# Deriving due times of the first groups' layers and weights from their users in a four-layer graph network

## The chip, the cores and the metric

The kernel runs on one core of one Trainium2 chip. The metric is the device time of one execution in microseconds (us); lower is better. Before the change it is 1435.51 us, the median of 3 runs (1435.34 to 1436.21). A core has a matrix engine (TensorE, PE in the profile, with its weight loads shown apart as PEld), a vector engine (VectorE, DVE), an activation engine (ScalarE, ACT), GpSimd (POOL), and SyncE (SP), whose queue issues the loads and stores here.

## The reference, cut to what matters

The input is 128 graphs of 64 nodes with 256 features, each with its own 64x64 adjacency. Four layers follow each other, each in the form x = x + layer(relu(layernorm(x)), adj):

```python
# layer 0: attention with 4 heads        e = leaky_relu(e_src_i + e_dst_j); masked softmax; alpha @ (h W); elu
# layer 1: the same with one head
# layer 2: relational convolution; adj holds only 0 and 1, so one relation of 40 is left:
#          (adj^T == 1) @ ((h W^T + b) * sigmoid(h W^T Wg^T + bg)), then relu
# layer 3: three steps of a gated recurrence with shared gates
for i in range(3):
    m = einsum("bnd,de->bne", h, weight[i])
    aggr = einsum("bst,bsd->btd", A, m)
    h = gru_cell(aggr, h, w_ih, w_hh, b_ih, b_hh)
```

All arithmetic is in float32. No graph needs another one, so the order of the graphs is free.

## The kernel before

Two graphs fill the 128 partitions, and four such pairs form a group (G = 4): 16 groups of 512 rows. For each group the kernel runs `first_layer`, `second_layer` (both call `attention`, line 1097) and `third_layer` (`loop_relation`, line 1187), then `before` (layernorm and transposes for the recurrence, line 739) and `recur` (`recurrence`, line 757: three steps with two halves of the features each). Groups 0 and 1 go through the layers in two halves of two pairs. For them layernorm's transposes run on PE; later groups (`g >= AHEAD`, line 1003) transpose by DVE and DMA. The second half of group 0 uses buffers of its own, with names that end in `e`.

The weights are prepared at the start. `later_weights` (line 1161) makes `wl` for the third layer from W_loop and Wg_loop (tiles `wn`, `gn`), `whh` from `hhn`, and for each of the three steps `wc`, a product of the transposed step weight (`gT`) and the transposed input weight (`ihT`). The step weights are loaded into `wrn0` and into the single buffers `wn` and `gn`, which they share with W_loop and Wg_loop: whichever load comes second waits until the first one's readers are done. The recurrence's buffers take the memory of the preparation (`make_gru`, line 1238), so all preparation and the halves of group 0 with an `e` must be done before recurrence 0 places a tile.

The code does not issue instructions in the order in which it is written. `Plan` (line 208) records each operation with an estimated cost, and `emit` (line 267) writes them out by list scheduling. It keeps a clock for each engine and takes the operation that can start first; where several of one engine are ready, it takes the one with the earliest due time (`key = (t, op.due)`, line 333). A result that another engine needs counts as ready `LATENCY` ns after its end. Each operation belongs to a job, opened by `begin`. A job with a start and an end spreads its operations' due times over that stretch; a job without an end counts back from the users:

```python
            if op.job.end is None:
                op.due = min((t.due for t in op.then), default=1e9) - op.cost
            else:
                op.due = (op.job.end - (op.job.end - op.job.start) * op.tail / op.job.length) * 1e3
```

The stretches are written by hand from line 1253 on: the weights from 18.0 to 79.1 us, the layers of groups 0 and 1 in `units`, recurrence g from `start + g * period` with start 93.6 and period 83.8. The chip then runs each engine's list in this fixed order.

Where the planner sees PE wait before 115 us, it puts filler products of a constant tile there (`nc.spare`, line 1315, `ni<-warm` in the profile). Their bank `ni` is later one of the five PSUM banks that only the recurrence uses (`Banks`, line 953); until a recurrence places its first tile in one of those five, the flag `early` is true and other tiles may use four of them.

In the profile nearly every instruction has line 384, the helper that records operations; products issued as a bundle have line 605. So tiles tell them apart: `mm<-w0e`, `mm<-w1e` and `mm<-wl` are the layers' products, `mm<-ihT,gT` makes wc, and `ry`, `rm`, `rz`, `nh`, `ni` belong to the recurrence.

Of the kernel before, what the change touches and what calls it, by code (L numbers as in the profile page):

```python
# [20 lines left out]
G = 4  # L21
# [27 lines left out]
class View:  # L49


    def __init__(self, base, shape, steps=(), region=None, live=None):
        self.base, self.shape, self.steps, self.region, self.live = base, tuple(shape), steps, region, live
# [83 lines left out]
class Pool:  # L137
# [3 lines left out]
    psum = False  # L141
# [21 lines left out]
    def released(self, tag, base, before):  # L163
# [3 lines left out]
        if before < 0:  # L167
            return 0.0
        return sorted(b.end for b in live if not b.left)[before] + Plan.LATENCY

# [29 lines left out]
class Job:  # L200
# [2 lines left out]

    def __init__(self, start, end, after):
        self.start, self.end, self.after, self.left, self.length = start, end, after, 0, 0.0


class Plan:

    LATENCY = 164.2

    def __init__(self, nc):
        self.nc, self.on, self.ops, self.job = nc, False, [], None
# [51 lines left out]
    def emit(self):  # L267
# [19 lines left out]
            op.job.length = max(op.job.length, op.tail)  # L287
        for op in reversed(self.ops):
            if op.job.end is None:
                op.due = min((t.due for t in op.then), default=1e9) - op.cost  # L290
            else:
                op.due = (op.job.end - (op.job.end - op.job.start) * op.tail / op.job.length) * 1e3
        free = dict.fromkeys([*ENGINES.values(), "-"], 0.0)
# [5 lines left out]
        def enter(op):  # L299
            t = 0.0  # L300
            for other, data in op.after.items():
                late = other.end + self.LATENCY
                if other.engine == op.engine and not (other.dma and data):
# [9 lines left out]
        while left:  # L313
            best = None
            for e, ops in ready.items():
                found = None
                for op in ops:
                    t = max(free[e], op.ready)
# [5 lines left out]
                    for b in op.needs:  # L324
                        if b.real is None:
# [5 lines left out]
                            t = max(t, b.pool.released(tag, b, taken.count(tag)))  # L331
# [7 lines left out]
            t, _, op, places = best  # L339
# [34 lines left out]
class Engine:  # L374
# [3 lines left out]
    def __getattr__(self, method):  # L378
        plan, engine = self.plan, self.name
        do = getattr(getattr(plan.nc, engine), method)  # L380

        def call(*args, **kwargs):
            def emit():
                return do(*[real(a) for a in args], **{k: real(v) for k, v in kwargs.items()})  # L384

            if not plan.on:
                return emit()
            writes = [v for v in args[:1] if isinstance(v, View)]
            reads = [v for v in [*args[1:], *kwargs.values()] if isinstance(v, View)]
            plan.note(  # L390
                ENGINES[engine], emit, cost(engine, method, args, kwargs), writes, reads,
                port=port(engine, method, writes, reads), dma=method == "dma_start",
            )

        return call
# [45 lines left out]
def kernel(  # L441
# [28 lines left out]
    nc = Plan(tc.nc)  # L470
# [128 lines left out]
    def beside(products, cost):  # L599

        def emit():
            for product in products:
                nc.nc.tensor.matmul(*[real(x) for x in product], start=True, stop=True)  # L605

        if not nc.on:
            return emit()
        writes = list({id(x[0].base): x[0] for x in products}.values())
        nc.note("PE", emit, cost, [Plan.all_of(x) for x in writes], [x for p in products for x in p[1:]])  # L610
# [337 lines left out]
    with ExitStack() as s1:  # L948
# [34 lines left out]
        psum = Banks(s1.enter_context(tc.tile_pool(name="psum", bufs=1, space=PSUM)), 1, Banks.own)  # L983
# [29 lines left out]
        def load_group(g):  # L1013
            nc.begin(("load", g))
            xg = work.tile([P, G, D], F32, name="xg", bufs=6)
            n = 2 if g == 0 else G
            for p in range(0, G, n):
                nc.sync.dma_start(xg[:, p : p + n], xr[:, g * G + p : g * G + p + n, :])
            at = work.tile([P, G // 2, 2, N], I32, name="at", bufs=3)
            for a in range(2):  # L1020
                for u in range(G // 2):
                    edges = tr[g * G // 2 + u, a]
                    nc.sync.dma_start(at[a * N : (a + 1) * N, u], edges)
            AT.append(at)
            XG.append(xg)
# [131 lines left out]
        def first_weights():  # L1157
            attention_columns(w0e, H, (AB[:, 0, :], AB[:, 1, :]))
            attention_columns(w1e, 1, (AB[:, 2, :], AB[:, 3, :]))
# [82 lines left out]
        def before(g):  # L1242
            ABD[g] = work.tile([P, G, N], F32, name="abd")
            START[g] = before_recurrence(W[3], psum, XG[g], AG[g], ABD[g], g >= AHEAD)

        def recur(g):
            recurrence(
                W[3], psum, START.pop(g), XG[g], ABD[g],
                lambda h, part: nc.sync.dma_start(outr[:, g * G : (g + 1) * G, :][part], h[part]),
                g == NG - 1,  # L1250
            )

        nc.begin("columns")
        first_weights()
        nc.begin("weights", 18.0, 79.1)
        later_weights(early)
        layers = (first_layer, second_layer, third_layer)
        start, period = 93.6, 83.8
        users = {}
        for g in range(NG):  # L1260
            if g > 1:
                load_group(g)

            if g == 0:
                units = [(0, 2, (-2.5, 24.3, 61.4, 71.1)), (2, 2, (-2.7, 25.3, 58.8, 74.4))]
            elif g == 1:
                units = [(0, 2, (27.5, 54.4, 87.5, 95.7)), (2, 2, (45.3, 71.4, 100.6, 129.4))]
            elif g == 2:
                units = [(0, G, (72.8, 119.1, 176.7, 238.7))]
            else:  # L1270
                end = start + g * period - 26.2
                units = [(0, G, [end - 53.5 * i + x for i, x in ((3, 0.0), (2, 0.0), (1, 0.0), (0, 0.0))])]
            for p0, n, at in units:
                spare = g == 0 and p0 > 0
                for i in range(3):
                    nc.begin((g, p0, i), at[i], at[i + 1], [users[i]] if i in users and not spare else [])
                    if not spare:
                        users[i] = (g, p0, i)
                    layers[i](g, p0, n, spare)
            if g == 0:  # L1280
                nc.begin("make")
                nc.note("-", make_gru, 0.0, [], [], [op for op in nc.ops if any(b.pool is early for b in op.bases)])
            at = start + g * period
            nc.begin(("before", g), at - (13.0 if g == 0 else 22.3), at, [("recur", g - 2)] if g > 1 else [])
            before(g)
            nc.begin(("recur", g), at, at + period)
            recur(g)
# [23 lines left out]
        if 115.0:  # L1311
            warm = const.tile([P, P], F32, name="warm")
            nc.nc.vector.memset(warm, 1.0)
            pause = psum.real.tile([P, P], F32, name="ni", tag="ni", bufs=1)
            nc.spare = lambda: nc.nc.tensor.matmul(pause, warm, warm, start=True, stop=True)  # L1315
        with tc.manual_schedule(engines={getattr(mybir.EngineType, e) for e in ENGINES.values()}):
            nc.emit()

# [214 lines left out]
```

## Time and profile before

| | us |
|---|---|
| time, median of 3 | 1435.51 |
| span of the profiled execution | 1432.5 |
| PE idle in the first 100 us | 2.06 |
| first product of recurrence 0 (ry) | 112.98 |
| first product of recurrence 1, of 2 | 197.12, 280.55 |
| last recurrence's last product starts | 1421.83 |

The span is the time from the first to the last instruction of one profiled execution on this core. The page gives busy time of each engine, the granted clock of PE in 40 slices, the chain of waits that ended last, and groups of instructions by line, operation and tile. Other views of the same trace show stretches of time, the order of instructions, or who waited for whom. A float32 product is two records (passes) in the trace, while the program has one instruction; counts after "x" in the profile are records unless a line says otherwise. Ends of products are modelled, so neighbouring products overlap in the records; the distance between starts gives the time that a product takes in a row of products.

### The profile page before, as it was taken

What the parts mean: (1) busy time and instruction counts of PE and PEld (TensorE: products, weight loads), DVE (VectorE), ACT (ScalarE), POOL (GpSimd) and SP (SyncE); (2) the same over time, 40 slices, a digit from 0 to 9 for tenths busy, and PEclk for the clock granted to TensorE, in tenths of its full rate; (3) what the DMA queues carried; (4) which work ended last, traced back from release to release, by engine and by line L of the source; (5) the groups of instructions that cost most, each with busy time, mean ns of one, the idle gap of its engine ahead of it and who ended that gap; (6) DMA issues with size and microseconds to landing.
All of it is one profiled execution on the core that took longest, in us unless ns stands there. A gap on an engine that the chain in (4) does not pass through costs nothing.

```text
span 1432.5 us, 28063 instructions
## 1 busy us (share of the span) xinstructions
PE 1412.5 (99%) x9779; PEld 973.6 (68%) x9779; DVE 1041.5 (73%) x2745; ACT 778.7 (54%) x1853; POOL 597.7 (42%) x744
## 2 busy tenths in 40 slices
PE   9999999999999999999999999999999999999997
PEld 9676676666667666666766666676666667666664
DVE  5568688686867878686887868688686868774544
ACT  3654655555565565556555555655655555554543
POOL 1424624534434453443445344344534434452422
PEclk9999999999999999999999999999999999999999
DMA  7010221222223122222312222231212222110000
GB/s 214 19 27 24 38 60 30 47 53 52 60 43 75 28 51 54 52 60 44 77 25 51 54 52 60 43 76 27 46 39 48 46 42 58 25 34 15 16 16 18
DMA packets 299421, 67.91 MB, mean 47 GB/s; under 512 B 274696, under 2 KB 297480, under 8 KB 299272
## 3 DMA queue, kind: packets, MB, share of 16 engines
q1 hardware_dynamic: 298712, 65.50, 21.7%
q8 instruction: 81, 1.33, 0.4%
q10 hardware_dynamic: 560, 0.52, 0.1%
q14 instruction: 68, 0.56, 0.1%
HBM read 28.06 MB, written 8.53 MB: 26 GB/s over the span
## 4 chain that ended last, share of the span: by engine, by line
PE 88%; DVE 4%; SPq 3%; ACT 3%; DMA 1%; issue 1%; POOL 1%; DVEq 0%; POOLq 0%; ACTq 0%
PE ry L384 22%; PE mm L384 16%; PE rz L384 11%; PE ni L384 11%; PE nh L384 10%; PE rm L384 5%; PE tp L384 4%; PE mm L605 3%; SPq L384 3%; PE tp L605 2%; PE ni L1315 2%; DVE d L384 1%; POOL d L384 1%; DVE hT L384 1%; DMA t<-row 1%
## 5 line engine op out<-in xcount | busy, mean ns | idle before, releaser
L384 POOL TENSOR_TENSOR d<-hT,t 128x256 f32<-128x256 f32 x192 | 151.9, 798 | 487.7 <-ACT t L384 486.8
L384 PE MATMUL ni<-aT,wc 128*128 128x512 f32 x384 | 194.1, 592 | 0.0
L384 PE MATMUL nh<-hT,whh 128*128 128x512 f32 x384 | 193.8, 593 | 0.2 <-DVE hT L384 0.2
L384 ACT ACTIVATE z<-z,brz 128x256 f32<-128x256 f32 x192 | 97.4, 507 | 155.9 <-DVE z L384 155.3
L384 DVE SCALAR_TENSOR_TENSOR d<-z,d 128x256 f32<-128x256 f32 x192 | 127.2, 669 | 58.1 <-POOL d L384 45.2
L384 POOL TENSOR_TENSOR hS<-hT 128x256 f32<-128x256 f32 x96 | 73.9, 770 | 175.5 <-PE ry L384 136.3
L384 ACT COPY z<-ry 128x256 f32<-128x256 f32 x192 | 71.2, 371 | 126.4 <-PE ry L384 91.2
L384 DVE SCALAR_TENSOR_TENSOR t<-r,t 128x256 f32<-128x256 f32 x192 | 98.0, 511 | 50.2 <-ACT r L384 44.5
L384 DVE TENSOR_TENSOR z<-rz,z 128x256 f32<-128x256 f32 x192 | 80.2, 418 | 59.1 <-PE rz L384 46.6
L384 PE MATMUL rz<-hS,whh 128*128 128x256 f32 x384 | 119.5, 393 | 1.1 <-DVE z L384 1.0
L384 PE MATMUL mm<-wl,hT 128*128 128x512 f32 x248 | 118.1, 598 | 0.0
L384 PE MATMUL ry<-hS,wsum 128*128 128x256 f32 x384 | 115.9, 383 | 0.8 <-ACT z L384 0.8
L384 PE MATMUL rz<-aS,wc 128*128 128x256 f32 x384 | 115.6, 383 | 0.0
L384 PE MATMUL ry<-aS,wsum 128*128 128x256 f32 x384 | 114.2, 379 | 0.0
L384 ACT ACTIVATE hn<-xg,var,rstd 128x256 f32<-128x256 f32 x200 | 107.1, 592 | 9.9 <-DVE var L384 9.8
L384 ACT ACTIVATE t<-t,bi 128x256 f32<-128x256 f32 x192 | 93.8, 502 | 19.8 <-DVE t L384 19.2
L384 PEld LDWEIGHTS ry<-hS,wsum 128*128 128x128 f32 x384 | 70.0, 190 | 47.0 <-issue 32.0
L384 DVE BATCH_NORM_STATS2 st<-xg 128x6 f32<-128x256 f32 x256 | 98.5, 413 | 3.2 <-DMA xg<-in_x_dram 2.5
L384 DVE SCALAR_TENSOR_TENSOR hT<-d,t 128x256 f32<-128x256 f32 x192 | 91.9, 485 | 6.1
L384 POOL TENSOR_TENSOR rstd<-var,mhalf 128x4 f32<-128x4 f32 (+1 forms) x70 | 68.7, 984 | 56.4 <-DVE var L384 47.4
L384 PEld LDWEIGHTS nh<-hT,whh 128*128 128x128 f32 x384 | 70.1, 190 | 27.3 <-issue 17.4
L384 PEld LDWEIGHTS ry<-aS,wsum 128*128 128x128 f32 x384 | 73.0, 190 | 22.7 <-issue 10.3
(203 smaller groups left out, 3227.6 us busy)
## 6 DMA issues: line engine op xcount, KB each, us to landing
hT<-hn SPq DMA_DIRECT2D x896, 32.0 KB
xg<-in_x_dram SPq DMA_DIRECT2D x15, 512.0 KB
out_dram<-hnat SPq DMA_DIRECT2D x15, 512.0 KB
t<-row SPq DMA_DIRECT2D x28, 256.0 KB
at<-in_adj_dram SPq DMA_DIRECT2D x64, 32.0 KB
eg<-in_adj_dram SPq DMA_DIRECT2D x64, 32.0 KB
ag<-in_adj_dram SPq DMA_DIRECT2D x16, 128.0 KB
t<-row SPq DMA_DIRECT2D x28, 64.0 KB
```

The source lines that it names most:

```text
L384: return do(*[real(a) for a in args], **{k: real(v) for k, v in kwargs.items()})
L605: nc.nc.tensor.matmul(*[real(x) for x in product], start=True, stop=True)
L1315: nc.spare = lambda: nc.nc.tensor.matmul(pause, warm, warm, start=True, stop=True)
```

## The change

Due times of the weights and of the layers of groups 0 and 1 are no longer spread over hand-written stretches. Their jobs have no end now, so each operation is due as late as its users allow, counted back through the operations to the recurrences, whose stretches keep fixed times. In the count, the cost of each operation, and LATENCY where the user sits on another engine, are multiplied by 1.76 (`spread`). The start is now 86.2 and the period 83.85, LATENCY 170.8, and the dates of the later groups are set anew. Filler products are emitted only while `early` is true, so that none is written into a bank of a recurrence.

```diff
         self.start, self.end, self.after, self.left, self.length = start, end, after, 0, 0.0
+        self.spread = 1.76
...
-    LATENCY = 164.2
+    LATENCY = 170.8
...
             if op.job.end is None:
-                op.due = min((t.due for t in op.then), default=1e9) - op.cost
+                op.due = 1e9
+                for t in op.then:
+                    late = 0.0 if t.engine == op.engine else self.LATENCY
+                    op.due = min(op.due, t.due - op.job.spread * (op.cost + late))
...
-        nc.begin("weights", 18.0, 79.1)
+        nc.begin("weights", 18.0, 0 or None)
...
-        start, period = 93.6, 83.8
+        start, period = 86.2, 83.85
...
             elif g == 1:
-                units = [(0, 2, (27.5, 54.4, 87.5, 95.7)), (2, 2, (45.3, 71.4, 100.6, 129.4))]
+                units = [(0, 2, (24.1, 54.4, 87.6, 97.3)), (2, 2, (45.5, 67.3, 98.2, 128.1))]
             elif g == 2:
-                units = [(0, G, (72.8, 119.1, 176.7, 238.7))]
+                units = [(0, G, (81.61, 124.36, 176.69, 239.68))]
             else:
-                end = start + g * period - 26.2
-                units = [(0, G, [end - 53.5 * i + x for i, x in ((3, 0.0), (2, 0.0), (1, 0.0), (0, 0.0))])]
+                end = start + g * period - 30.69
+                units = [(0, G, [end - 52.62 * i + x for i, x in ((3, 0.0), (2, 0.0), (1, 0.0), (0, 0.0))])]
...
-                    nc.begin((g, p0, i), at[i], at[i + 1], [users[i]] if i in users and not spare else [])
+                    end = None if g < 2 else at[i + 1]
+                    nc.begin((g, p0, i), at[i], end, [users[i]] if i in users and not spare else [])
+                    if g > 1:
+                        nc.job.spread = 3.0
...
-            nc.begin(("before", g), at - (13.0 if g == 0 else 22.3), at, [("recur", g - 2)] if g > 1 else [])
+            nc.begin(("before", g), at - (13.0 if g == 0 else 21.1), at, [("recur", g - 2)] if g > 1 else [])
...
-            nc.spare = lambda: nc.nc.tensor.matmul(pause, warm, warm, start=True, stop=True)
+            nc.spare = lambda: psum.early and nc.nc.tensor.matmul(pause, warm, warm, start=True, stop=True)
```

## The prediction

> **What bounds the kernel now.** I read the busy table of the whole page first, then the row of the granted clock.
>
> ```profile
> span 1432.5 us, 28063 instructions
> ...
> PE 1412.5 (99%) x9779; PEld 973.6 (68%) x9779; DVE 1041.5 (73%) x2745; ACT 778.7 (54%) x1853; POOL 597.7 (42%) x744
> ...
> PEclk9999999999999999999999999999999999999999
> ```
>
> TensorE (PE) is busy 99% of the span at full clock, and the chain of waits gives it 88%. So the end comes nearer only if PE has less to do or stands still less. Next I cut the span at the period of the recurrences, some 84 us.
>
> ```profile
> 0.00:100.00 100.00, 97.94 (x719) 76.95 (x720) 62.06 (x223) 48.61 (x128) 32.06 (x54) 1.00 0.33 90
> 100.00:184.00 84.00, 82.33 (x652) 55.46 (x651) 57.84 (x158) 47.30 (x117) 38.31 (x50) 1.00 0.15 30
> 184.00:268.00 84.00, 83.94 (x524) 57.24 (x523) 64.87 (x172) 46.97 (x113) 30.44 (x38) 1.00 0.23 48
> 351.00:435.00 84.00, 83.94 (x583) 57.25 (x582) 65.23 (x170) 47.22 (x112) 37.15 (x46) 1.00 0.25 52
> 1357.00:1433.00 76.00, 63.72 (x365) 43.26 (x363) 33.14 (x75) 32.65 (x74) 21.47 (x29) 0.95 0.05 16
> ```
>
> Columns: stretch, length, then busy time of PE, weight loads, DVE, ACT, POOL. A middle period leaves PE 0.06 us idle of 84; the losses lie at the two ends. But the start is fuller than it is useful: the line that makes the filler products shows what "busy" means there.
>
> ```profile
> L1315 PE MATMUL ni<-warm x318: 272/275/582, 1.1 to 102.5; 128*128 128x128 f32 x159
> ```
>
> These 159 filler products (two passes each in the records) compute nothing. The planner puts them where it foresees that PE waits. The timeline gives their price: 28 passes follow each other from 12.18 to 15.30 us, 0.111 us a pass, 0.223 us a product; 50 passes from 29.23 to 34.92 give 0.228.
>
> Why does PE wait there? In the timeline and the table of waits, between 40 and 75 us:
>
> ```profile
> 41.87 1.99 PE L384 MATMUL mm<-ihT,gT 128*128 128x512 f32 x4
> 44.35 1.88 PE L384 MATMUL mm<-ihT,gT 128*128 128x512 f32 x4
> 46.06 1.94 PE L384 MATMUL mm<-w0e,hT 128*128 128x264 f32 x8
> DVE es L384 <- PE mm L384: 10.0, 5, 7.2
> ```
>
> Group 0's and group 1's layer products stand in the PE queue behind products that prepare the recurrences' weights (mm<-ihT,gT). DVE has nothing for 7.2 us, and later, from 88 to 100 us, PE runs 32 fillers while DVE catches up with the last layers of group 0. Recurrence 0 starts (first ry) at 112.98 us.
>
> **What the skill says.** The page "Perfetto Trace Analysis", at its top, calls matmul busy time a bad measure because matmuls are pipelined, and points to the weight loads' share. The trace agrees: PEld is 68% where PE is 99%, and part of the 99% is filler. "TensorE: Matmul & The Clock Gate" (The HAM clock gate) says that an idle window of about 3.4 us halves the PE clock. No run here shows such a drop; the row above has full clock throughout. It matters because the change removes fillers only where products take their place, and 119 remain. The same page (Specifications table) has ACT, DVE and GpSimd as strict first-in first-out; the 7.2 us in which DVE waits at one es copy fits that, and it is why an order that is wrong by one entry costs.
>
> **The change, part by part.** All counts are from the two programs' instruction orders.
>
> 1. Total work: on DVE, ACT, POOL and the DMA queue every kind of instruction has the same count before and after. On PE one kind differs: fillers fall from 159 to 119. 40 x 0.223 = **8.9 us** less on the engine that bounds (9.1 at 0.228).
>
> 2. Group 0 and the weights: the loop-relation weights (wl) now come first, the recurrence's weights (wc) fill the gaps of group 0's layers. From the first wl product to the first ry the order before has 33 fillers, the new one 15, so 18 of the 40 fall there; the rest go from the first layers. Group 0's last layer comes sooner.
>
> 3. Recurrence 0 starts sooner. Before its first ry 8 products with w0e, 4 with w1e, 4 with wl and 8 transposes less are queued, all of groups 1 and 2. By the timeline 4 products with w0e take 1.78 us, 4 with w1e 1.80, a pass of 128x512 0.43, a transpose 0.11: 3.56 + 1.80 + 3.44 + 0.88 + 0.4 of small ones = 10.1 us. With the fillers 19.0 us: ry at about 94 us. But these 10.1 us are moved, not saved. Recurrence 1 stands 15.6 us earlier in the PE order, recurrence 2 8.5, recurrences 3 to 10 exactly 9.0, all of it filler: from there on the same work lies ahead. So only the 8.9 us can reach the end.
>
> 4. Idle time given back. Between the starts of recurrences 0 and 1 DVE gets 41 instructions more (161 to 202): six statistics (0.41 us each), two more each of the three 128x512 steps of attention (0.70 each), bias and gate of two more pairs, and small ones; by the rows' means 14.3 us. From 116 to 200 us DVE was busy 64.4 of 84; now 78.7 of about 88, 90%. What PE loses beside a full DVE shows here:
>
> ```profile
> 120.00:130.00 10.00, 10.00 (x100) 7.13 (x99) 9.83 (x34) 4.76 (x10) 0.71 (x1) 1.00 0.00 1
> 130.00:140.00 10.00, 10.00 (x42) 5.79 (x44) 9.38 (x21) 5.04 (x13) 6.47 (x6) 1.00 0.01 2
> 140.00:150.00 10.00, 8.65 (x95) 4.99 (x92) 9.77 (x36) 6.56 (x15) 7.08 (x9) 1.00 0.03 5
> ```
>
> In 30 us with DVE 97% busy PE lost 1.35 us, 4.5%. Over 82 us that is 3.7 us, the upper end; the lower is 0, since PE has the moved work of groups 1 and 2 to fill with. I take the middle, 1.9 us.
>
> 5. Fillers now stop with the first bank of a recurrence. A wait after that would be bare idle time and not a missing filler, so some of the 40 may be waits still there. Before, none came after 102.5 us, though allowed to 115. Within the 1.9.
>
> 6. Loads: the single buffers wn and gn now hold the loop weights first, and two recurrence weights are loaded after their transposes. The SP queue waits there, ahead of loads for groups 2 and later. Those transposes are the 18th to 45th rows of PE's order (about 20 to 24 us); the late weights are used behind another 37 us of products. A load of this size took about 3 us before (wn issued at 56.54, its bytes through by about 59.2 in the DMA row). Cost 0, hidden by those products.
>
> 7. LATENCY 170.8, the later group 2 dates and the earlier dates of groups 3 to 15 leave each kind's count between recurrences 3 and 10 alone: 0 us. At recurrences 14 and 15 the order shifts by +1.7 and -1.3 us of work, which is moved: 0, give or take 1.3. spread is read only for jobs without an end, so 3.0 for later groups does nothing.
>
> Sum: -8.9 - 0.1 + 1.9 = **-7.1 us**: 1435.5 - 7.1 = 1428.4.
>
> **Rivals.** A, nothing is given back, and the tail has its 1.3 us: 1435.5 - 9.0 = 1426.5, at best 1425.2. For it: PE's idle time in the first 100 us before is only 2.06 us, so the plan fits the chip. B, DVE and the tight dates of group 1 return more: group 1's last layer now ends only some 20 us of PE work ahead of recurrence 1, where before it had 60. With the 3.7 us of step 4 and as much again at recurrence 1: 1435.5 - 9.0 + 7.4 = 1433.9, or 1431 to 1433 for a part. C, everything comes back as idle time in place of fillers, because waits and not the order set recurrence 1: 1435.5. D, slower: DVE becomes the bound from recurrence 0 to 1, all of its 14.3 us stretch the stage and only 9.0 are gained: 1435.5 + 5.3 = 1440.8. Against C and D: 9 us of DVE idle time remain in that stage, and DVE idled 38 us in the first 100, some of which earlier layers now use.
>
> **The numbers.** The forecast and its neighbourhood (1427 to 1431) 0.48, A 0.22, B 0.16, C 0.07, D 0.07. Faster by 0.2% means under 1432.6: forecast, A and most of B, 0.85; same 0.08; slower 0.07. The range takes A's best end and B's upper part: 1425.0 to 1433.0.
>
> **What would show it.** Fillers x238 in the records. First ry near 94 us. From recurrence 3 each start 5 to 9 us earlier than before (280.55 us for recurrence 2's first ry is the mark nearest), the middle periods unchanged. PE idle time from 94 to 185 us up to 3.7 us, next to DVE at 90%. It is wrong if PE shows several us of idle time on DVE between recurrences 0 and 1, if it waits for a late weight before 94 us, or if the middle periods lengthen.

## The result and the profile after

The changed kernel takes 1441.75 us (median of 4 runs, 1440.87 to 1442.04), the kernel before 1435.86 beside it (4 runs, 1435.34 to 1437.37). The ratio is 1.0038, 95% interval 1.0021 to 1.0056: **slower by 0.4%**, where 1428.4 us was forecast.

The page's head, and below it the row of fillers, in the same views as before:

```profile
span 1439.4 us, 27884 instructions
...
PE 1408.9 (98%) x9699; PEld 968.5 (67%) x9699; DVE 1049.2 (73%) x2745; ACT 777.2 (54%) x1853; POOL 596.7 (41%) x744
```

```profile
L1322 PE MATMUL ni<-warm x238: 273/275/581, 1.1 to 90.3; 128*128 128x128 f32 x119
```

PE is busy 3.6 us less than before and the span is 6.9 us longer, so PE stands still some 10 us more: 1439.4 - 1408.9 = 30.5 us idle against 20.0. The fillers are the 119 that were forecast; that PE's busy time falls by 3.6 us and not by their 8.9 means that the remaining products take some 5 us longer in the records. The same stretches of the span as in the prediction, and the last one from recurrence 15 on:

```profile
0.00:100.00 100.00, 98.47 (x740) 74.60 (x741) 67.12 (x226) 52.30 (x135) 38.49 (x61) 1.00 0.34 92
100.00:184.00 84.00, 81.99 (x526) 54.63 (x524) 60.61 (x174) 47.78 (x119) 31.15 (x40) 1.00 0.14 28
184.00:268.00 84.00, 81.85 (x632) 55.67 (x632) 62.94 (x161) 46.11 (x108) 38.09 (x45) 1.00 0.25 52
351.00:435.00 84.00, 83.50 (x581) 57.16 (x580) 65.25 (x169) 46.39 (x111) 35.17 (x45) 1.00 0.24 51
1363.00:1439.40 76.40, 64.89 (x369) 44.16 (x367) 33.27 (x76) 32.25 (x74) 21.64 (x29) 0.95 0.05 16
```

The first row is better than before, the second much the same; the third and fourth are worse (PE idle 2.15 and 0.50 us where it was 0.06 in each). The fourth is a piece of the steady part. One whole period, from the first ry of recurrence 6 to that of recurrence 7, of before (first row) and after (second row), from the same view:

```profile
614.28:697.63 83.35, 83.30 (x582) 57.08 (x581) 64.34 (x169) 46.77 (x112) 36.74 (x45) 1.00 0.25 52
```

```profile
612.90:698.10 85.20, 83.85 (x582) 57.45 (x581) 65.48 (x169) 46.63 (x112) 36.40 (x45) 1.00 0.25 51
```

The counts in brackets are equal but for one ACT record at the edge: the same instructions take 1.85 us more, and PE idles 1.35 us where it idled 0.05. This repeats. The starts of recurrences in the timelines (first ry, us), with the mean period between recurrences 3 and 13:

| first ry of recurrence | 0 | 1 | 2 | 3 | 13 | mean period | span |
|---|---|---|---|---|---|---|---|
| before | 112.98 | 197.12 | 280.55 | 363.92 | 1199.82 | 83.59 | 1432.5 |
| after | 91.57 | 182.28 | 274.51 | 358.87 | 1206.86 | 84.80 | 1439.4 |
| after less before | -21.41 | -14.84 | -6.04 | -5.05 | +7.04 | +1.21 | +6.9 |

At recurrences 2 and 3 the change is 5 to 6 us ahead. Then ten periods of 1.21 us more turn -5.05 into +7.04, and the tail adds nothing. Over these ten periods PE idles 9.7 us where before idles 1.8, and its records of the same products are 4.2 us longer. So the question is what lengthens a period in which nothing was added.

The waits of PE name it. First before, the three largest, then after; columns are total us, times, longest:

```profile
PE tp L384 <- DVE hT L384: 4.9, 5, 2.6
PE ry L384 <- ACT aT L384: 2.7, 3, 0.9
PE rm L384 <- DVE r L384: 1.1, 3, 0.4
```

```profile
PE mm L609 <- issue: 5.6, 8, 1.1
PE rz L388 <- DVE z L388: 3.6, 11, 0.5
PE tp L388 <- DVE hT L388: 3.4, 4, 2.6
PE mm L609 <- PE ry L388: 2.4, 3, 0.9
```

Line 609 is a bundle of small products (line 605 before). Two rows of it are new, 8 + 3 times and 8.0 us together: once in a period PE stands ahead of the second layer's bundle, `mm<-wh,t` with 64x257 (7.2 us in the ten periods from recurrence 3 to 13, and nothing in before). In the timeline of PE after:

```profile
678.99 0.59 PE L388 MATMUL rm<-aT,wc 128*128 128x256 f32 x2
680.63 0.40 PE L609 MATMUL mm<-wh,t 64*64 64x257 f32 x1 [1.04 <-issue]
```

"issue" says only that the profile shows no releaser. The bundle reads `t`, so I followed t: DVE multiplies it by gd and masks it by mt, and waits for the DMA that spreads a row over the partitions (t<-row, two loads; I call them the spreads, they have nothing to do with the planner's `spread`). The timelines of DVE, before and after:

```profile
677.56 0.43 DVE L384 TENSOR_TENSOR t<-t,gd 128x256 f32<-128x256 f32 x1 [1.40 <-DMA t<-row]
```

```profile
678.97 0.43 DVE L388 TENSOR_TENSOR t<-t,gd 128x256 f32<-128x256 f32 x1 [1.95 <-DMA t<-row]
```

Both kernels wait for the DMA. Before, the product stands 63.3 us behind the period's first ry, the mask ends at 679.11, and PE has products queued up to the bundle's start at 680.36: 1.25 us in hand. After, the product stands 66.1 us behind the first ry, 2.8 us later, and PE has run dry. (The mean over the ten periods is 63.5 and 65.6 us, 2.0 later.) Why later? SyncE's queue, the start and length of its issues, before and after:

```profile
670.92 1.34 SPq L384 DMA_DIRECT2D eg<-in_adj_dram  x2
672.36 0.44 SPq L384 DMA_DIRECT2D row<-fT  x1
672.84 1.25 SPq L384 DMA_DIRECT2D eg<-in_adj_dram  x2
674.19 1.19 SPq L384 DMA_DIRECT2D t<-row  x2
```

```profile
669.77 2.62 SPq L388 DMA_DIRECT2D eg<-in_adj_dram  x4
672.48 0.44 SPq L388 DMA_DIRECT2D row<-fT  x1
673.03 1.31 SPq L388 DMA_DIRECT2D hT<-hn  x2
674.43 2.29 SPq L388 DMA_DIRECT2D t<-row  x2
```

An issue of these sizes costs the queue some 0.65 us (the row 0.44). After the change all four loads of edges (eg, used only by the third layer) stand ahead of the row, where two did, and between the row and its spreads come two transposes (hT<-hn): two issues more ahead of the spreads. The spreads are issued 61.5 us behind the first ry instead of 59.9. In this period the first of them also holds the queue 1.66 us instead of 0.55. That isn't a wait for the row, whose semaphore was complete at 674.04, before the queue came to the spread at 674.43; issues of 1 to 2 us turn up now and then among the edge loads, the transposes and the spreads of both kernels (before has one of 1.59 on the same load, two periods later), and no run shows why. The remaining 1.6 us come from when the queue gets to the row and from what it issues between the row and the spreads. DVE's copy of the row (fT), which the row's DMA waits for, before and after:

```profile
671.19 0.27 DVE L384 COPY fT<-tp 4x128 f32<-4x128 f32 x1
```

```profile
671.42 0.24 DVE L388 COPY fT<-tp 4x128 f32<-4x128 f32 x1
```

The copy was done at 671.66 after the change, and the queue came to the row at 672.48: the row waits for its turn. But the copy itself comes later too, it ends 58.8 us behind the first ry instead of 57.2, because DVE now does a large transpose ahead of it. So both DVE's order and the queue delay the row, and only experiments can tell them apart.

From here on my theory was: the later groups' dates (-30.69, 52.62), not the early ones, change the repeating order; what it costs is paid through the place in SyncE's queue. The rival ideas were that the start itself is at fault (DVE, late weights), or that DVE's order around its transposes is.

### The profile page after: what moved, and what is told of

It is laid out like the page before. It is cut to its first block, busy times and chain, and to the rows that moved or that the text cites. A ratio compares the mean times of both kernels' runs of the same rounds, so it can differ in the third digit from the quotient of the medians.

```text
span 1439.4 us, 27884 instructions
## 1 busy us (share of the span) xinstructions
PE 1408.9 (98%) x9699; PEld 968.5 (67%) x9699; DVE 1049.2 (73%) x2745; ACT 777.2 (54%) x1853; POOL 596.7 (41%) x744
## 4 chain that ended last, share of the span: by engine, by line
PE 87%; DVE 4%; SPq 3%; ACT 3%; issue 1%; DMA 1%; POOL 0%; POOLq 0%; ACTq 0%; DVEq 0%
PE ry L388 21%; PE mm L388 17%; PE nh L388 11%; PE ni L388 10%; PE rz L388 10%; PE rm L388 5%; PE tp L388 4%; PE mm L609 3%; PE tp L609 3%; SPq L388 3%; PE ni L1322 2%; DVE t L388 1%; DVE d L388 1%; PE tq L609 1%; ACT hn L388 1%
## 5 line engine op out<-in xcount | busy, mean ns | idle before, releaser
L388 POOL TENSOR_TENSOR d<-hT,t 128x256 f32<-128x256 f32 x192 | 145.1, 765 | 468.9 <-ACT t L388 467.5
L388 DVE SCALAR_TENSOR_TENSOR t<-r,t 128x256 f32<-128x256 f32 x192 | 109.6, 576 | 55.3 <-ACT r L388 47.7
L388 POOL TENSOR_TENSOR hS<-hT 128x256 f32<-128x256 f32 x96 | 79.1, 827 | 168.3 <-PE ry L388 122.9
L388 DVE SCALAR_TENSOR_TENSOR d<-z,d 128x256 f32<-128x256 f32 x192 | 103.1, 545 | 39.1 <-POOL d L388 25.4
L388 POOL TENSOR_TENSOR aS<-aT,aS 128x256 f32<-128x256 f32 x96 | 72.3, 753 | 51.4 <-ACT aT L388 48.0
L388 POOL TENSOR_TENSOR hS<-hT,hS 128x256 f32<-128x256 f32 x96 | 74.4, 775 | 44.0 <-DVE hT L388 36.6
L388 PEld LDWEIGHTS rz<-hS,whh 128*128 128x128 f32 x384 | 70.2, 190 | 25.8 <-DVE z L388 7.9
```

## The experiments

All are compared with the kernel before, run beside them. Its own median moves between 1434.6 and 1435.9 us from one batch of runs to another, so small differences between experiments are read from the ratios (given with their 95% intervals) and from the traces.

### e1, e2: the two halves of the change

e1 is the kernel after with the later parts put back:

```diff
-    LATENCY = 170.8
+    LATENCY = 164.2
-        start, period = 86.2, 83.85
+        start, period = 86.2, 83.8
-                end = start + g * period - 30.69
-                units = [(0, G, [end - 52.62 * i + x for i, x in ((3, 0.0), (2, 0.0), (1, 0.0), (0, 0.0))])]
+                end = start + g * period - 26.2
+                units = [(0, G, [end - 53.5 * i + x for i, x in ((3, 0.0), (2, 0.0), (1, 0.0), (0, 0.0))])]
-            nc.begin(("before", g), at - (13.0 if g == 0 else 21.1), at, [("recur", g - 2)] if g > 1 else [])
+            nc.begin(("before", g), at - (13.0 if g == 0 else 22.3), at, [("recur", g - 2)] if g > 1 else [])
```

> The changed kernel with LATENCY 164.2, period 83.8, the later groups' dates (end - 53.5 * i, - 26.2) and the 22.3 us ahead of a recurrence as they were before; the new due times of the weights and of groups 0 and 1, the start at 86.2 and group 2's new dates stay. By the instruction orders every recurrence period from the fifth on is then word for word that of the kernel before, with 123 fillers. Theory 1 (the first two groups' new order gains some 6 us up to recurrence 2, and the later groups' new dates lose it again, about 1.2 us in each period): recurrence 0 near 92 us, periods 83.4 to 83.6, and 1428 to 1431 us in all, faster than before by 5 to 7. Theory 2 (the loss comes from the new start, as a shift of the recurrences against their loads or as something that persists): periods stay near 84.8 and the time near 1441. Theory 3 (DVE between recurrences 0 and 1 is what costs): the time stays at 1436 or above because recurrences 1 and 2 come no earlier than before.

e2 is the kernel before with the later dates alone:

```diff
-                end = start + g * period - 26.2
-                units = [(0, G, [end - 53.5 * i + x for i, x in ((3, 0.0), (2, 0.0), (1, 0.0), (0, 0.0))])]
+                end = start + g * period - 30.69
+                units = [(0, G, [end - 52.62 * i + x for i, x in ((3, 0.0), (2, 0.0), (1, 0.0), (0, 0.0))])]
```

> The kernel before with one line's edit: the later groups' dates of the changed kernel (- 30.69 and 52.62 in place of - 26.2 and 53.5). The start, its 159 fillers and the hand-set stretches stay. From recurrence 6 on its PE order is that of the changed kernel. Theory 1: recurrence 0 at 113 us as before, periods 84.6 to 85.1 from recurrence 6 on, so 10 to 13 us slower than before: 1445 to 1449. Theory 2: periods of 83.4 and the time of before, 1435 to 1437.

Measured: e1 1441.11 us (ratio 1.0041, 1.0028 to 1.0055), e2 1453.9 (1.0137, 1.0121 to 1.0153). Starts of recurrences 0 to 3 and 13, and the mean period:

| | 0 | 1 | 2 | 3 | 13 | mean period 3 to 13 |
|---|---|---|---|---|---|---|
| e1 | 91.41 | 185.85 | 281.05 | 373.04 | 1207.13 | 83.41 |
| e2 | 114.07 | 198.19 | 281.40 | 369.32 | 1219.06 | 84.97 |

The periods follow the later dates: 83.4 with the old ones, 85.0 with the new ones, whatever the start (from recurrence 6 to 13 alone 84.7 in e2 and 84.9 in after). The order of PE in e2 is that of after from recurrence 6 on, that of e1 is before's from recurrence 5 on. So the period's loss belongs to the dates. Both totals were missed. e1's start was as early as after's, and the first three periods (94.4, 95.2, 92.0 us) gave back what it had gained. e2 is 5 us above its range; its periods from recurrence 2 to 5 (87.9, 85.8, 86.9 us), where the old dates meet the new ones, are longer than either kernel's. That became a second question, taken up under e4.

### e3, e3b: does the row's landing set the wait?

In both kernels the spread of layer 1 (the second attention layer) reads a fixed row of the input instead of the row just written, so it needn't wait for the row's DMA; its place in the queue stays.

```diff
+                    to = t[half * N : (half + 1) * N].rearrange("p c i -> p (c i)")
+                    if layer == 1:
+                        fixed = bass.AP(tensor=xr.tensor, offset=xr.offset, ap=[[0, N], [1, nh * N]])
+                        nc.note(
+                            "SP", lambda to=to, fixed=fixed: nc.nc.sync.dma_start(to.real(), fixed),
+                            nh * N * N * 4 / 150.0, [to], [row[half : half + 1, :]], dma=True,
+                        )
+                    else:
+                        nc.sync.dma_start(to, row[half : half + 1, :].to_broadcast([N, nh * N]))
```

> The changed kernel, with every order as it is; only in the second attention layer of groups 2 and later the two loads of t read a fixed row of x in place of the row that DVE and a store have just made, so they wait for nothing (the values of that layer's attention are then others). Theory 1a (in each period PE stands about 1.2 us at the second layer's bundle of products, because t arrives at 678.97 where the bundle could start at 679.4, and DVE's three steps follow): that stall goes, periods fall from 84.8 to about 83.7, and the time falls by 10 to 13 us, to 1429 to 1432. Theory 1b (the longer periods come from many small waits of a worse order on PE and DVE, the bundle being only where they show): the bundle's wait moves elsewhere, periods stay at 84.3 or more, the time at 1436 to 1441.

> The same loads of a fixed row in the kernel before: the control. There PE does not wait at the second layer's bundle, so both theories expect 1433 to 1436 us, a change of at most 2 us.

Measured: e3 1443.06 us (1.0053, 1.004 to 1.0067), mean period 84.72; e3b, the control, 1434.25 (0.9996, 0.9988 to 1.0004). e3's time is above the ranges of both theories. The gap ahead of the bundle shrank from 1.04 to 0.68 us in the period shown, and from 7.2 to 6.4 us over the ten periods; the waits of PE kept it (6.8 us on "issue"). So the landing isn't it, as the semaphore times above say too: the spread's own issue comes late, behind what stands ahead of it in the queue.

### e5, e5b, e6: fewer issues ahead of the row

The order of every engine stays; only the edge loads of a group become two instead of four. They bring other graphs' edges, untransposed, so the third layer's values are others (the expectations say second layer, but eg is read by the third alone).

```diff
-                    nc.sync.dma_start(eg[r * N : (r + 1) * N, 2 * u : 2 * u + 2], er[g * G // 2 + u, r])
+                    both = eg[r * N : (r + 1) * N]
+                    first = 2 * g * G + r * G
+                    source = adj[first : first + G].rearrange("b j i -> j b i")
+                    def load(both=both, source=source, r=r, g=g):
+                        if (g, r) not in LOADED:
+                            LOADED.add((g, r))
+                            nc.nc.sync.dma_start(both.real(), source)
+                    nc.note("SP", load, 2 * N * N * 4 / 150.0, [to], [], dma=True)
```

> The kernel after, with the instruction order on every engine as it is; from group 2 on the four loads of edge indices of a group (eg, two for each half) become two loads of twice the size. They take the edges of other graphs and untransposed, so the values of the second layer differ from the reference. On SyncE's queue two issues fewer (half of the 2.62 us that the four take at 669.77) then stand ahead of the row and of its two spreads. Theory 1 (the place of row and spreads in SyncE's queue sets the new wait ahead of the second layer's bundle): the spreads are issued 1.3 us sooner, the product of t and gd starts near 677.7 instead of 678.97, the 0.93 us of PE idle ahead of the bundle go, the period falls from 84.8 to about 83.9 us and eleven to thirteen periods give 10 to 12 us back: 1430 to 1432. Rival (VectorE's order around the transposes sets it, the queue is slack): the wait moves but the period stays within 0.25 us, what the fixed row gave: 1439 to 1442.

> The same merging of the edge loads in the kernel before, a control for its own cost: with it the values of the second layer differ from the reference. There PE never waits ahead of the second layer's bundle, so both theories expect the periods of before, 83.4 to 84.0 us, and the time of before within 0.2%: 1434 to 1437.

> e5_merged_edges and e3_fixed_row together: after's order, the edges merged into two loads (with the values that this gives) and layer 1's spreads reading a fixed row of the input rather than the row just written. It asks what the remaining 0.5 us of e5's periods (83.9 against 83.4) are. If the row's own transit still sets the product of t and gd, taking the wait for the row away brings the period to 83.4 to 83.6, 1428 to 1431; if the rest is the order of VectorE and ScalarE, the periods stay at 83.9, 1433 to 1435.

Measured: e5 **1433.69 us** (0.9989, 0.9981 to 0.9997), 8.1 us less than after by the times and 7.0 by the ratios; e5b 1433.38 (0.9985, 0.9978 to 0.9992), 2.2 less than before. SyncE's queue, DVE and the waits of PE in e5, for the same place in the period:

```profile
667.13 1.32 SPq L1051 DMA_DIRECT2D eg<-in_adj_dram  x2
668.92 0.27 SPq L388 DMA_DIRECT2D row<-fT  x1
669.30 1.31 SPq L388 DMA_DIRECT2D hT<-hn  x2
670.70 1.20 SPq L388 DMA_DIRECT2D t<-row  x2
```

```profile
674.46 0.42 DVE L388 TENSOR_TENSOR t<-t,gd 128x256 f32<-128x256 f32 x1 [0.20 <-DMA t<-row]
```

```profile
PE tp L388 <- DVE hT L388: 3.7, 4, 2.6
PE rz L388 <- DVE z L388: 3.6, 11, 0.5
```

The queue now waits for the row's copy and not the copy for the queue (the gap between 668.45 and 668.92; the copy ends at 668.88), DVE waits 0.20 us instead of 1.95, and both bundle rows are gone from PE's waits: 8.0 us there. The gap shows what the Trainium skill, "DMA: Bandwidth & Descriptors" (Anatomy of one DMA — SWDGE (gpsimd) path), says of any DMA: its semaphore wait happens on the issuing sequencer before dispatch. The transposes behind the row stood still with it. The copy ends 58.8 us behind the first ry as in after, and the spreads are issued at 60.6: in this period 1.0 of the 1.6 us was the queue, the rest goes with DVE's later copy.

The mean period is 83.94, as expected: 0.86 us of the 1.21 are back; the time is 1.7 us above what was expected. The control gained as well, 2.2 us (just under its range), and its mean period goes from 83.59 to 83.39; what is after's own is at least the difference, 5 to 6 us of the 7 to 8. With the queue relieved in both kernels their times are equal, but not their periods: 0.55 us of the 1.21 still part them, and the 7 us by which e5 is ahead of e5b at recurrence 3 pay for it. So SyncE's queue is shown as the cause of PE's wait ahead of the bundle, and of a little over half of what the periods differ by.

The rest is not the landing: e6, with the fixed row as well, has 1434.25 us (0.9999, 0.999 to 1.0007) and the same 83.94. What stays in after, e5 and e6 alike is rz<-DVE z, 3.4 to 3.6 us in ten or eleven waits of 0.3 us, where before has 1.0 in two. That is 0.26 us in a period, about half of the remaining 0.55; that it comes from DVE's changed order is read from the trace, not tried, and the other half stays open.

### e9: the edges on another queue

The same cure with all values kept: after's order, the edge loads issued by ScalarE.

```diff
-                    nc.sync.dma_start(eg[r * N : (r + 1) * N, 2 * u : 2 * u + 2], er[g * G // 2 + u, r])
+                    to, source = eg[r * N : (r + 1) * N, 2 * u : 2 * u + 2], er[g * G // 2 + u, r]
+                    if g < AHEAD:
+                        nc.sync.dma_start(to, source)
+                    else:
+                        nc.note(
+                            "SP", lambda to=to, source=source: nc.nc.scalar.dma_start(to.real(), source),
+                            2 * N * N * 4 / 150.0, [to], [], dma=True,
+                        )
```

> The kernel after, in its own order and with all values as they were; from group 2 on the four edge loads of a group are issued from ScalarE's queue instead of SyncE's. Theory 1 (SyncE's queue ahead of the row and the spreads is what lengthens the periods): as with merged loads and a little more, since all four issues (2.62 us) leave the queue; periods 83.4 to 84.0 instead of 84.8, time 1429 to 1434. Rival (the issues cost ScalarE, whose r and z stand on the recurrence's path, what SyncE gains): 1436 to 1442.

Measured: 1435.06 us (1.0002, 0.9993 to 1.001), mean period 84.04. The waits on "issue" are gone here too, and the total is that of before: the earlier start pays for periods that are still 0.45 us longer. The time is 1 us above what was expected. The skill's "DMA: Bandwidth & Descriptors" (Rules for kernel authors) says that spreading DMAs over issuing engines brings no bandwidth and only saves the sequencer's issue time. Here that issue time was the whole point.

### e4a, e4b: the hand-over from the new start to the old dates

e1 kept group 2's new dates beside the old ones of groups 3 to 15. e4a and e4b change only these in e1:

```diff
-                units = [(0, G, (81.61, 124.36, 176.69, 239.68))]
+                units = [(0, G, (65.4, 111.7, 169.3, 231.3))]     # e4a
+                units = [(0, G, (72.8, 119.1, 176.7, 238.7))]     # e4b
```

> The kernel after with the early edits kept (ranked weights, new dates of groups 0 and 1, the start of 86.2) and the later groups put back to what they were (-26.2, 53.5, the 22.3 us of the window before a recurrence, period 83.8, LATENCY 164.2); unlike the first experiment, group 2 gets the old dates moved with the start: 65.4, 111.7, 169.3, 231.3. From recurrence 5 on the order of a period is then that of before. Theory 1 (the 17 us that the first experiment lost between recurrences 1 and 3 came from group 2's new dates not fitting the old later ones): the periods go to 83.4 us at the latest from recurrence 4, the hand-over costs under 5 us, and what the start gained stays: 1426 to 1431, faster than both kernels. Rival (any hand-over from the crowded start to the old later dates costs it): 1436 to 1442.

> As e4a_group2_shifted, but with group 2's dates as in the kernel before, not moved with the start: 72.8, 119.1, 176.7, 238.7. Theory 1: the second layer of group 2 is dated 5 us sooner than with the new dates and the first 9 us sooner, so most of the loss goes as well: 1427 to 1433, with the hand-over worth 0 to 3 us more than in e4a. Rival: 1436 to 1442 for both.

Measured: e4a 1437.36 us (1.0011, 1.0004 to 1.0017), e4b **1432.67** (0.9975, 0.9964 to 0.9986). Recurrence 3 starts at 367.02 and 363.80, against 373.04 in e1. e4b is within its theory's range, e4a within its rival's. Group 2's dates do matter, with 6 and 9 us, but e4a, which I held for the better, is the worse one, and the hand-over still costs more than the 3.9 us of after: relative to before, PE time that neither queued work nor fillers explain is 17 us at recurrence 3 in e1, 11 in e4a and 8 in e4b. I get this from the starts: change of start, less the fillers dropped before it, less the products moved across it.

### e8, e10: changing over later

After's dates for groups 2 to 4, before's from group 5 on, LATENCY at 164.2; e10 with the edges on ScalarE as in e9.

```diff
+                late, step = (30.69, 52.62) if g < 5 else (26.2, 53.5)
+                end = start + g * period - late
+                units = [(0, G, [end - step * i + x for i, x in ((3, 0.0), (2, 0.0), (1, 0.0), (0, 0.0))])]
...
+            nc.begin(("before", g), at - (13.0 if g == 0 else (21.1 if g < 5 else 22.3)), at, [("recur", g - 2)] if g > 1 else [])
```

> The kernel after with LATENCY at 164.2 and the later groups' dates changed over in two stages: group 2 as in the kernel after, groups 3 and 4 with its -30.69, 52.62 and 21.1, and from group 5 on the -26.2, 53.5 and 22.3 of the kernel before. From recurrence 6 on the order of every engine in a period is that of before. Theory 1 (the early edits are worth what the prediction said, the later dates lose it): 40-odd fillers fewer give 9 us, the periods from recurrence 5 on are 83.4, and the hand-over between recurrences 1 and 5 costs 3 to 6 us: 1428 to 1433, and faster than the hand-over with group 2's old dates. Rival (a change-over of dates costs 8 us or more wherever it is put): 1433 to 1440.

> e8_graded with the edge loads on ScalarE's queue as in e9_act_edges: whether the two gains add. The merged loads took 2.2 us off the kernel before, whose later order this one has; so theory 1: 1 to 2.5 us less than e8_graded, 1426 to 1431. Rival (the issues on ScalarE cost as much as they free, where no wait for the spreads is left): as e8_graded or up to 3 us more.

Measured: e8 1435.61 us (1.0008, 0.9999 to 1.0016), e10 1436.05 (1.0004, 0.9996 to 1.0012): the rival in both. The periods of e8 settle at 83.35, but the hand-over costs 11 us before that. In e10 the issues on ScalarE bring nothing where nobody waits for the spreads: the periods are 83.6 and not 83.35. Not all of these 11 us are order: PE waits 3.96 us for DVE at 203.47 in e8 (4.01 in e10), and the granted clock is half of full from 206.56 to 213.39 (in e10 from 209.55 to 212.96). At half clock PE was busy 6.0 and 3.4 us, which costs half of that, 3.0 and 1.7 us. All 13 runs of e8 have a mean granted clock of 0.995 to 0.997, where before has 0.997 or 0.998.

### e11, e12: a pause and its clock

In e4b the hand-over has a visible piece, the one that e8 and e10 have too. PE waits 3.1 us for DVE ahead of the first bundle of group 3's first layer, at 208.24. The wait, and the stretches of 4 us behind its start (the third number from the right is the granted clock):

```profile
208.24 0.37 PE L609 MATMUL mm<-wh,t 64*64 64x65 f32 x1 [3.10 <-DVE t L388]
```

```profile
206.00:210.00 4.00, 1.76 (x34) 1.56 (x35) 3.69 (x10) 0.51 (x1) 0.00 (x0) 0.68 0.32 53
210.00:214.00 4.00, 4.00 (x41) 2.87 (x40) 2.65 (x10) 1.06 (x2) 0.20 (x1) 0.50 0.14 24
```

The clock is half from 207.45 to 214.28, and from 208.24 on PE is fully busy: (214.28 - 208.24) x 0.5, so the clock alone costs 3.0 us. e11 puts 12 fillers into the wait, e12 six; they go into a bank that the bundle overwrites.

```diff
-    def beside(products, cost):
+    def beside(products, cost, fill=None):
         def emit():
+            for _ in range(12 if fill is not None else 0):       # e12: 6
+                nc.nc.tensor.matmul(real(fill), nc.warm, nc.warm, start=True, stop=True)
...
+            late = u == 0 and nc.jobs.get((3, 0, 0), 0) is nc.job
-            beside(products, 710.0 if heads > 1 else 660.0)
+            beside(products, 710.0 if heads > 1 else 660.0, banks[0][:, :P] if late else None)
```

> The kernel of e4b_group2_old in its own order, with 12 matmuls of the constant filler (128x128, 0.22 us each, into a bank that the bundle overwrites) put into TensorE's queue ahead of the first bundle of group 3's first layer, which waits 3.1 us for VectorE at 208.24. In e4b_group2_old the granted clock falls to 0.68 and 0.50 in the two stretches of 4 us after 206, and the hand-over from recurrence 1 to 3 costs 7 us more PE time than before. Theory 1 (the pause lets the clock down, and that is half of the loss): with the pause filled the clock stays at 1.00 through this window, the second period falls from 93.1 to 89 to 90 us and the time to 1428.5 to 1430. Rival (the clock falls for the stretch of small tiles and the waits around it, or the loss is queued work): clock and period as they are, 1432 to 1434.

> As e11_pause_filled, with 6 fillers (1.3 us) instead of 12: the last 1.8 us of the wait stay idle. Theory 1: if a pause of under 2 us is borne without a lower clock, as the 1 us pauses of the kernel after are, the same gain as with 12; if the clock is granted by the idle share, part of it, 1429 to 1432. Rival: as e4b_group2_old, 1432 to 1434.

Measured: e11 **1430.55 us** (0.9969, 0.9958 to 0.998), e12 **1430.60** (0.9971, 0.9961 to 0.9981), faster than before by 0.3% and, by the ratios, than after by 0.7%. Against e4b it is 2.1 us by the times and 0.6 to 0.9 by the ratios, whose intervals overlap; the traces are clearer. The same stretches of e11, and the wait that remains in e12:

```profile
206.00:210.00 4.00, 3.35 (x52) 2.80 (x50) 4.00 (x11) 0.51 (x1) 0.00 (x0) 1.00 0.32 53
210.00:214.00 4.00, 4.00 (x49) 2.99 (x48) 3.73 (x10) 2.64 (x5) 0.73 (x1) 1.00 0.13 22
```

```profile
204.06 1.50 PE L609 MATMUL mm<-warm 128*128 128x128 f32 x12
207.32 0.27 PE L611 MATMUL mm<-wh,t 64*64 64x65 f32 x1 [1.75 <-DVE t L388]
```

DVE is as late as ever (the bundle starts 19.6 us behind recurrence 1 in all three), but the clock stays at 1.00, and here a rest of 1.75 us idle does no harm. The second period is 90.9 us in e11 and 91.0 in e12 instead of 93.1, a little less gained than the 3 to 4 us expected. So some 2 us of the hand-over in e4b's trace were the clock after a pause; the other 6 are not settled. That e4b's median gains less than its trace has a reason on record: three of its seven runs have a mean granted clock of 0.995 or 0.996 and take 1433.4 to 1434.7 us (the profiled one among them), the other four have 0.997 or 0.998 and take 1429.6 to 1432.7. All 16 runs of e11 and e12 have 0.997 or 0.998, and take 1429.6 to 1432.9. The clock falls in some executions of e4b and not in others. The 6 us lie between recurrences 1 and 3, where the order of three mixed groups differs from kernel to kernel, and no run takes one single wait out of it. e4a loses 11 us there without a fall of the clock; of e1's 17, two falls of the clock (from 218.26 and from 303.59) make up 4.8.

## Why the prediction was wrong

1. **The fillers**: 159 to 119, as said; 8.9 us less work. Right.
2. **The order of group 0 and the weights**: wl first. The first ry says how much it brought: 91.57 us, where about 94 was forecast. Right, and 2.4 us sooner still; where these come from stays open, and they are gone again at recurrence 1.
3. **Recurrence starts**: step 3's work plus step 4's 1.9 us gave recurrence 1 15.6 - 1.9 = 13.7 us sooner and recurrence 2 8.5 - 1.9 = 6.6 sooner; measured 14.84 and 6.04. Right within 1.2 us, and the remark that most of the early gain is moved work holds. At recurrence 3 it was to be 7.1 and is 5.05: 2 us more were given back on the way than was said.
4. **Idle time given back**: 1.9 us were taken. From recurrence 0 to 1 PE is busy 88.70 of 90.71 us, 2.0 idle; but before idles 1.7 us in the same stage (82.47 of 84.14), so only 0.3 us are new, and by the starts 15.6 - 14.84 = 0.8 us were given back. That the idle time comes near the forecast is luck, and the reason is wrong: DVE was to be 90% busy there and is 70% (63.91 of 90.71), with 180 instructions in the records where before has 173. Counting instructions between two marks in the orders of two engines doesn't tell what runs between two times.
5. **Fillers stopping with the first bank, and the loads (6)**: up to 94 us PE's waits are 1.1 us for the fillers' own tile and 0.2 us, less than the 1.8 us of before in its first 113. Right.
7. **"leave each kind's count between recurrences 3 and 10 alone: 0 us"**: this is the step that failed. The counts are equal, as it says (582 products in either period), but their order isn't, on PE, VectorE, ScalarE and SyncE alike. It cost 12.1 us from recurrence 3 to 13. 7.2 of it were PE's wait ahead of the second layer's bundle, another 1.3 the bundle itself (0.72 us instead of 0.59 from its start to the next product's); e5 took both away by shortening SyncE's queue. The order of the repeating period was put at nothing, and it set when a late load was issued. The tail, 0 give or take 1.3, was right: +7.04 at recurrence 13 and +6.9 at the end.

Put together: the sum was -7.1, the chip had -5.05 at recurrence 3, and the term priced at zero was +12. Rival D gave 1440.8, near the result by luck, by a mechanism (DVE as the bound from recurrence 0 to 1) that the trace contradicts. What was missing is a rival for the steady part. The prediction's own list named the sign, "the middle periods lengthen", but put no chance on it. The evidence was there to be read: the two programs' orders show four eg loads ahead of row in SyncE's list instead of two, and the trace of before shows DVE waiting 1.40 us for t<-row there, with 1.25 us in hand ahead of the bundle.

One reading of the trace was wrong as well: the prediction has full clock throughout, but its own last row has 0.95. The clock of before is half from 1425.4 us on, near the end of the program. It had no part in the result, but a row of nines (90% or more each) can't show that a clock never fell.

## What to carry to other kernels

Equal counts of instructions are no price of zero. When a scheduler's dates move, compare the orders of a repeating period on every queue, the DMA-issuing one too, and look in the old trace for chains that are nearly late: a loss of 1 us there is multiplied by the periods, while what a better start gains comes once. Where PE must wait some 3 us, fillers keep its clock; half the wait filled was enough here.

## What the runs showed of the hardware

In e4b the granted clock fell to half during one TensorE pause of 3.1 us and stayed there for 6.8 us, 6.0 of them full work; with half the pause filled, 1.75 us idle, it didn't fall (e12). The skill's "TensorE: Matmul & The Clock Gate" (The HAM clock gate) gives an idle window of about 3.4 us. The length is in the traces, but the window need not be idle. But e1's clock fell as well, at 218.26, with single waits of no more than 1.2 us: in a stretch of 4 us PE was busy 2.12 us, much of it with bundles of 64-row tiles. The stretch and the next one:

```profile
216.00:220.00 4.00, 2.12 (x54) 1.59 (x46) 3.76 (x11) 2.20 (x4) 1.59 (x3) 0.78 0.32 53
220.00:224.00 4.00, 4.00 (x25) 2.32 (x27) 4.00 (x11) 1.28 (x3) 4.00 (x3) 0.50 0.31 51
```

In every trace the clock's record knows two values, full and half, and up to the last products its changes lie whole multiples of 3.41 us apart (e4b and e8 twice that at half clock, e10 once). Cut on this grid, the first 1410 us of the 16 traces have 8 stretches at full clock in which PE is busy less than half of the 3.41 us; a fall follows 6 of them, one of them in e3 with waits of only 0.74 and 1.03 us. It follows one other stretch of them all, at 58%: e1's, with the 64-row bundles. After has the same two waits as e3, but they lie in two stretches, and its clock stays; so, too, with the 1.75 us of e12. So the busy share of a stretch goes with the fall, and not an unbroken pause alone, and the same wait may cost the clock in one execution and not in the next; no run varied that share by itself.

And a DMA issue has a price on the queue that issues it, some 0.65 us each on SyncE for edges and for transposes alike, and the same for a load of twice the size (two in 1.32 us, where four took 2.62); about one in thirty of these took 1 to 2 us, for no reason that a run shows. Halving the edge loads took 2.2 us off before, in whose PE waits I had found nothing that pointed at them.
